# Softplus additions as accumulating transfers, and GpSimd's share of the product with B, in a four-layer network kernel

## The chip, the cores and the metric

The kernel runs on one core of a Trainium2 chip. The metric is the device time of one execution in microseconds (us). The core has five engines that run side by side, each with its own queue in order: TensorE (PE: matrix products, PEld: their weight loads), VectorE (DVE), ScalarE (ACT), GpSimd (POOL) and SyncE (SP, which here only issues DMA transfers). GpSimd issues DMA transfers too. Engines wait for each other and for transfers through semaphores.

## The reference

A feature map of 4 images x 256 channels x 64 x 64 goes through four residual layers, each `x = x + layer(groupnorm(x))`: a deformable convolution, a self-attention, a second deformable convolution with 16 groups, and a Mamba block. The change lies in the last, which is, cut to what matters:

```python
L, D_INNER, D_STATE = 4096, 512, 16                      # L = h * w positions
u, res = split(x_seq @ in_proj_w.T)                      # L x 512 each
u = silu(causal_conv4(u) + conv_b)
dt, Bm, Cm = split(u @ x_proj_w.T)                       # 16 columns each
delta = softplus(dt @ dt_proj_w.T + dt_proj_b)           # L x 512
deltaA = exp(delta[..., None] * A)                       # L x 512 x 16
deltaBu = delta[..., None] * Bm[:, None, :] * u[..., None]
state_t = deltaA_t * state_{t-1} + deltaBu_t             # scan over L
y_t = sum_n state_t[:, n] * Cm_t[n]
out = ((y + u * D) * silu(res)) @ out_proj_w.T
```

## The kernel before, in words

The images are worked off one after the other. For each, the layers `layer0` to `layer3` follow each other; they share only the tile `x`, which holds the image in SBUF (the on-chip memory of 128 partitions). All that follows is about `layer3`.

Positions lie along the free dimension, the 512 inner channels as 4 blocks (`dc`) of 128 partitions. The 4096 positions are cut into 8 chunks (`j`) of 512. In each chunk the 16 states (`n`) are worked off one after the other, so that an image has 128 steps `s = 16 j + n`. A step does this:

- TensorE makes `bn`: row n of B, spread over all partitions by a product with a selecting matrix, in PSUM (L1583). There is one such bank.
- VectorE multiplies it with `du` = delta x u into the tile `h` (`product`, L1598): 128 x 2048 elements. In a helped step it does three of the four blocks only, 128 x 1536; the fourth is `quarter` (L1590) on GpSimd, which reads the row of B from a tile `bs` that SyncE has spread over the partitions by a transfer two steps ahead (`ahead`, L1574), and writes `hq`.
- For each block, ScalarE makes `da = exp(delta x A)` (L1679) in one of two PSUM banks, and VectorE scans with it (L1681), with the running state from `carry`. The fourth scan of a helped step reads `hq` in place of `h`.
- GpSimd saves the scan's last column in `carry` (L1701) and multiplies `h` with the row of C (`cn`, L1704).
- TensorE sums `h` over the states into four PSUM banks `ys` (`add`, L1561), two steps late.

Which steps are helped is the list `helped`: states 14, 15 and 0 to 5, except 14 and 15 of chunk 0.

Beside the states of one chunk, the kernel prepares the next: `front(j)` lays its parts into slots of the steps of chunk j-1, and `close(j)` does the output of the chunk before. The order on TensorE, ScalarE, VectorE and GpSimd is the order in which the program issues the instructions, written out by hand; SyncE's is left to the scheduler. A slot is a pair of step and place in the step (0 and 1 between and after the scans, 2 after the product with C, -1 at the start). Front step k falls on step 16 (j-1) - 5 + k, so on state n = k - 5 of the chunk before; for j = 1, the front starts later and is packed closer.

The part of the front that matters is softplus, computed as relu(z) - (exp(-|z|) ...) with a logarithm. ScalarE writes `du = |z|` and `delta = relu(z)` (L1385, L1386), then `du = exp(-du)` (L1418), `w = du + 1` (L1422), `du = 1 - w` (L1427) and `w = ln(w)` (L1430), each over 128 x 2048. GpSimd adds `du` before and after L1427, which leaves the rounding error of w, and then `w`, to `delta` (L1433, three times), and at last makes `du = delta x u` (L1434), which the next chunk's products read. The first addition must have read `du` before L1427 writes it. For j = 1 the slots are packed closer:

```python
at = dict(e=(11, 0), w=(12, 0), c=(13, 1), ln=(14, 1), s=((11, 0), (12, 1), (15, 0)), sums=(11, 14, 16, 18))
if j == 1:
    at = dict(e=(10, 1), w=(11, 1), c=(12, 1), ln=(13, 0), s=((11, 0), (12, 0), (13, 1)), sums=(10, 12, 13, 15))
```

Here `e`, `w`, `c` and `ln` are the slots of ScalarE's four passes, `sums` the steps of the three additions and of du's product, and `s` those of `split`, which cuts the rows of B into bf16 parts and has a small subtraction on GpSimd twice (L1401, L1405).

The functions that the change touches, with the lines of the profile:

Of the kernel before, what the change touches and what calls it, by code (L numbers as in the profile page):

```python
# [13 lines left out]
ALU = mybir.AluOpType  # L14
# [14 lines left out]
DS = 16  # L29
# [34 lines left out]
class Net:  # L64
# [1068 lines left out]
    def layer3(self, x, out, nxt, early):  # L1133
# [7 lines left out]
        nc, tc = self.nc, self.tc  # L1141
        C = 512
        NC, LEAD = N // C, 5
        with (
# [166 lines left out]
            def front(j):  # L1311


                c = chunks[j]
                todo = []
                put = lambda step, half, pe, rest: todo.append((step, half, pe, rest))
# [112 lines left out]
                put(*at["c"], None, over)  # L1429
                put(*at["ln"], None, lambda: nc.scalar.activation(c["w"], c["w"], AF.Ln))  # L1430

                for step, part in zip(at["sums"], ("du", "du", "w")):
                    put(step, 2, None, lambda part=part: nc.gpsimd.tensor_add(c["delta"], c["delta"], c[part]))  # L1433
                put(at["sums"][3], 2, None, lambda: nc.gpsimd.tensor_mul(c["du"], c["delta"], c["u"]))  # L1434

                for dc in range(4):
# [124 lines left out]
                    nc.tensor.matmul(c["ys", dc], self.ident, h[:, dc, :], start=False, stop=(n == DS - 1))  # L1561


            hs, helped = {}, [s for s in range(NC * DS) if s % DS in (14, 15, 0, 1, 2, 3, 4, 5) and s // 2 != 7]

            def ahead(s):

# [35 lines left out]
            for j in range(1, NC):  # L1603
                for step, half, pe, rest in front(j):
                    at = DS * (j - 1) - (LEAD if j > 1 else 2) + step
                    if at >= 0:
                        slots.setdefault((at, half), []).append((pe, rest))
# [44 lines left out]
            with tc.manual_schedule(  # L1652
# [14 lines left out]
                for s in range(total):  # L1667
                    j, n = s // DS, s % DS
                    c = chunks[j]
# [179 lines left out]
```

## Time and profile before

| what | value |
|---|---|
| median of 3 runs | 9220.24 us (9211.65 to 9221.78) |
| the profiled execution, its own time | 9224.37 us |
| its span, first to last instruction | 9222.6 us |
| mean granted TensorE clock | 0.967 |
| busy: PE, DVE, POOL, ACT | 8204.3, 7308.7, 6976.5, 4967.0 us |
| layer 3 of image 0 (from 1432.1 to 2343.8 us) | 911.7 us |
| an ordinary chunk in it | 112.4 us |
| L1433, 84 additions of 128 x 2048 on GpSimd | 4.54 us each |
| L1590, 248 quarters on GpSimd | 1.27 us each |

The profile comes from one execution. Its page gives each engine's busy time, the groups of instructions by line with their mean duration and the idle time ahead of them, and the DMA queues; further views give single instructions in order of time, and busy times by stretch. A stretch table has, for each stretch, its length, the busy us of PE, PEld, DVE, ACT and POOL with the number of instructions, the granted clock, the share of the DMA engines and GB/s. In a timeline a row has the start, the duration, the engine, the line, the operation, what is written and read, and how many equal instructions were put together. Instructions that only issue a transfer count as no busy time, except for the gathers of layer 0 (L371), which GpSimd issues.

### The profile page before, as it was taken

The page shows a single profiled execution, that of the slowest core. Times are in us where ns is not written, and L with a number is a line of the kernel's source. Part 1 is how long each engine was busy: PE and PEld are TensorE (multiplying, and loading weights), DVE is VectorE, ACT ScalarE, POOL GpSimd, SP SyncE. Part 2 cuts the span into 40 slices and gives each one's busy share as a digit, 9 for nine tenths or more (in the row PEclk, how much of TensorE's full clock was granted, in tenths as well). Part 3 has the DMA queues.
Part 4 walks back from the last instruction along what each step waited for, and adds up shares of the span by engine and source line. Part 5 has one row for each costly group of instructions (what it writes and reads, how often), then busy time and mean ns, then how long its engine had stood idle before and what let it go on. Part 6 is the DMA issues. An engine that isn't in the chain of part 4 may idle for free. (4 is left out here: it accounts for less than half of the span.)

```text
span 9222.6 us, 95498 instructions
## 1 busy us (share of the span) xinstructions
PE 8204.3 (89%) x32023; PEld 4337.2 (47%) x32023; DVE 7308.7 (79%) x8245; ACT 4967.0 (54%) x7717; POOL 6976.5 (76%) x4224
## 2 busy tenths in 40 slices
PE   5889898998888989899888898999988889889997
PEld 4643473443564346344356435634435633564443
DVE  5864498999786458999978645899997854689998
ACT  4843336666684333666668333366666833336664
POOL 4746697998674669799867467889986746788997
PEclk9999999999999999999999999999999999999999
DMA  8930011222892011122389101112248900111221
GB/s 301 356 120 1 29 58 59 67 67 82 288 360 90 1 34 61 56 66 66 100 297 359 61 1 39 59 57 67 66 121 311 349 33 1 43 61 53 63 63 51
DMA packets 409192, 1017.79 MB, mean 110 GB/s; under 512 B 38833, under 2 KB 106834, under 8 KB 406642
## 3 DMA queue, kind: packets, MB, share of 16 engines
q0 software_dynamic: 165888, 604.05, 17.5%
q1 hardware_dynamic: 242802, 407.54, 14.4%
q8 instruction: 255, 4.18, 0.2%
q14 instruction: 247, 2.02, 0.1%
HBM read 849.60 MB, written 88.10 MB: 102 GB/s over the span
## 5 line engine op out<-in xcount | busy, mean ns | idle before, releaser
L1704 POOL TENSOR_TENSOR h<-h,cn 128x2048 f32<-128x2048 f32 x508 | 2300.4, 4528 | 41.1 <-POOL carry L1701 0.2
L1681 DVE TENSOR_TENSOR_SCAN h<-da,carry,h 128x512 f32<-128x512 f32 x1800 | 2175.2, 1265 | 85.0 <-ACT da L1679 36.8
L1679 ACT ACTIVATE da<-delta,l3a 128x512 f32<-128x512 f32 x2048 | 1395.7, 689 | 1206.4 <-DVE h L1681 1202.7
L1561 PE MATMUL y<-h,ident 128*128 128x512 f32 x4096 | 1923.7, 603 | 14.8 <-POOL h L1704 14.8
L371 POOL DMA_INDIRECT g<-tab,idx x1152 | 1337.0, 1161 | 515.3 <-DVE r L380 131.3
L592 POOL TENSOR_TENSOR acc<-acc,e 128x1024 f32<-128x1024 f32 x480 | 1125.4, 2345 | 540.0 <-ACT e L588 518.8
L1561 PEld LDWEIGHTS y<-h,ident 128*128 128x128 f32 x4096 | 787.7, 194 | 1067.6 <-issue 975.9
L415 PE MATMUL pz<-cols,l0w 128*128 128x256 f32 x4608 | 1154.8, 395 | 30.2 <-DVE cols L404 24.5
L489 DVE TENSOR_REDUCE m<-pm 128x3 f32<-128x1536 f32 (+2 forms) x340 | 599.5, 1763 | 699.6 <-PE pm L479 699.6
L380 DVE SCALAR_TENSOR_TENSOR r<-g,wx,r 128x512 f32<-128x512 f32 x1152 | 862.2, 748 | 238.0 <-ACT r L379 230.5
L588 ACT ACTIVATE e<-sc 128x1024 f32<-128x1024 f32 x512 | 496.1, 1020 | 1029.4 <-PE sc L575 1025.2
L1598 DVE TENSOR_TENSOR h<-du,bn 128x2048 f32<-128x2048 f32 (+1 forms) x512 | 1025.9, 2004 | 4.0 <-PE bn L1583 3.9
L599 PE MATMUL cx<-e,v 128*128 128x512 f32 x2048 | 1000.2, 616 | 0.0
L379 ACT ACTIVATE r<-g,wx 128x512 f32<-128x512 f32 x1152 | 830.0, 720 | 283.1 <-DMA g<-tab,idx 230.9
L415 PEld LDWEIGHTS pz<-cols,l0w 128*128 128x128 f32 x4608 | 857.9, 196 | 179.3 <-DVE cols L404 79.4
L888 DVE TENSOR_TENSOR prod<-ring,A 128x768 f32<-128x768 f32 (+1 forms) x640 | 716.6, 1161 | 90.0 <-DMA ring<-ring 59.3
L913 PE MATMUL pacc<-ident,prod 128*128 128x128 f32 x5120 | 678.8, 284 | 75.7 <-POOL prod L893 41.7
L397 PE MATMUL pt<-ident,acc 128*128 128x128 f32 x2304 | 437.2, 290 | 264.3 <-DVE acc L388 261.3
L913 PEld LDWEIGHTS pacc<-ident,prod 128*128 128x128 f32 x5120 | 576.7, 144 | 164.9 <-POOL prod L893 62.2
L599 PEld LDWEIGHTS cx<-e,v 128*128 128x128 f32 x2048 | 352.3, 189 | 599.0 <-issue 596.4
L387 ACT ACTIVATE acc<-r,wy 128x256 f32<-128x256 f32 x1152 | 569.2, 494 | 4.2 <-DVE r L380 3.1
L388 DVE SCALAR_TENSOR_TENSOR acc<-r,wy,acc 128x256 f32<-128x256 f32 x1152 | 551.7, 479 | 2.4 <-ACT acc L387 2.0
(272 smaller groups left out, 11488.7 us busy)
## 6 DMA issues: line engine op xcount, KB each, us to landing
cn<-cd SPq DMA_DIRECT2D x512, 256.0 KB
bs<-cd SPq DMA_DIRECT2D x248, 256.0 KB
tab<-vtnext SPq DMA_DIRECT2D x96, 512.0 KB
ring<-ring SPq DMA_DIRECT2D x288, 126.0 KB
ring<-ring SPq DMA_DIRECT2D x288, 124.0 KB
g<-tab,idx POOLq DMA_INDIRECT x1152, 6.3
tab<-vt SPq DMA_DIRECT2D x28, 640.0 KB
x<-in_x SPq DMA_DIRECT2D x64, 256.0 KB
```

The costliest lines, as they stand in the source:

```text
L371: nc.gpsimd.indirect_dma_start(out=g[:], out_offset=None, in_=tab[:, :], in_offset=bass.IndirectOffsetOnAxis(ap=idx[:, t, k : k + 1], axis=0),
L379: nc.scalar.mul(r, g[:, :, 0, :], wx[:, 0, t, k : k + 1])
L380: nc.vector.scalar_tensor_tensor(r, g[:, :, 1, :], wx[:, 1, t, k : k + 1], r, ALU.mult, ALU.add)
L415: nc.tensor.matmul(sums[m][:, ot, :256], wf[:, i, bass.ts(ot, P)], cols[m][:, i, :], start=(i == 0), stop=(i == 17),)
L592: nc.gpsimd.tensor_add(b["acc"], b["acc"], e)
L599: nc.tensor.matmul(blocks[qb]["cx"], v[:, 4 * (i + kt // 4 * 4) + kt % 4, :], e[:, bass.ts(i % 2, 512)], start=(kt == 0 and i == 0), stop= ...
L913: nc.tensor.matmul(d["pd"][:, ct, t, :], prod[:, x, t, bass.ts(ct, P)], self.ident, is_transpose=True, start=(wy == 0 and x == left[0] and ...
L1561: nc.tensor.matmul(c["ys", dc], self.ident, h[:, dc, :], start=False, stop=(n == DS - 1))
L1598: nc.vector.tensor_mul(h[:, :d, :], c["du"][:, :d, :], c.pop(("bn", n)).to_broadcast([P, d, C]))
L1679: nc.scalar.activation(da, c["delta"][:, dc, :], AF.Exp, scale=al[:, dc, n : n + 1])
L1681: nc.vector.tensor_tensor_scan(h[:, dc, :], da, hb, carry[:, dc, n : n + 1], ALU.mult, ALU.add)
L1704: nc.gpsimd.tensor_mul(h, h, cn.to_broadcast([P, 4, C]))
```

## The change

In the fronts of chunks 2 to 7, the three additions to `delta` become transfers that GpSimd issues, which add their source to what stands in `delta` (`accum_op=ALU.add`), each of 128 x 2048 elements, 1 MB. The front of chunk 1 keeps its three GpSimd additions. The product that makes `du` stays on GpSimd in all. The list of helped steps becomes: in chunks 1 to 7 all states but 13 and 14, in chunk 0 states 0 to 5.

```diff
@@ front(j) of layer3
+                def sum(part):
+                    if j == 1:
+                        nc.gpsimd.tensor_add(c["delta"], c["delta"], c[part])
+                    else:
+                        nc.gpsimd.dma_start(out=c["delta"], in_=c[part], accum_op=ALU.add)
+
                 for step, part in zip(at["sums"], ("du", "du", "w")):
-                    put(step, 2, None, lambda part=part: nc.gpsimd.tensor_add(c["delta"], c["delta"], c[part]))
+                    put(step, 2, None, lambda part=part: sum(part))
                 put(at["sums"][3], 2, None, lambda: nc.gpsimd.tensor_mul(c["du"], c["delta"], c["u"]))
@@ layer3
-            hs, helped = {}, [s for s in range(NC * DS) if s % DS in (14, 15, 0, 1, 2, 3, 4, 5) and s // 2 != 7]
+            hs, helped = {}, [
+                s for s in range(NC * DS) if (s // DS and s % DS not in (13, 14)) or s % DS in (0, 1, 2, 3, 4, 5)
+            ]
```

## The prediction

> **What bounds the kernel now.** I read the page first, then the stretch table cut at the start of each chunk of layer 3, then the timelines of VectorE, ScalarE and GpSimd in one chunk. Only layer 3 is touched, so only it is costed.
>
> ```profile
> L1704 POOL TENSOR_TENSOR h<-h,cn 128x2048 f32<-128x2048 f32 x508 | 2300.4, 4528 | 41.1 <-POOL carry L1701 0.2
> L1681 DVE TENSOR_TENSOR_SCAN h<-da,carry,h 128x512 f32<-128x512 f32 x1800 | 2175.2, 1265 | 85.0 <-ACT da L1679 36.8
> L1679 ACT ACTIVATE da<-delta,l3a 128x512 f32<-128x512 f32 x2048 | 1395.7, 689 | 1206.4 <-DVE h L1681 1202.7
> ```
>
> In these groups ScalarE waits 1202.7 us for VectorE's scans, while the scans waited 85 us for anything. The waiting goes towards VectorE. The stretch table (busy us of PE, PEld, DVE, ACT, POOL, count in brackets) says the same by chunk; the first two rows are ordinary chunks, the last is chunk 7 of image 0:
>
> ```profile
> 1887.20:1999.50 112.30, 106.70 (x253) 45.82 (x252) 110.84 (x87) 73.93 (x102) 105.26 (x49) 1.00 0.23 66
> 1999.50:2111.90 112.40, 106.81 (x253) 45.81 (x252) 110.94 (x87) 73.94 (x102) 105.37 (x49) 1.00 0.22 67
> ...
> 2224.30:2343.80 119.50, 89.64 (x243) 39.70 (x243) 114.72 (x99) 73.72 (x108) 88.34 (x42) 0.91 0.57 171
> ```
>
> VectorE is busy 110.9 of 112.4 us; the 1.5 us left are the 0.1 us between product and first scan, 16 times. It bounds the chunk. TensorE has 5.6 us idle, GpSimd 7.0, at a granted clock of 1.00.
>
> What a state costs VectorE, with and without GpSimd's quarter (the 128x1536 and the 128x2048 product):
>
> ```profile
> 1810.79 1.73 DVE L1598 TENSOR_TENSOR h<-du,bn 128x1536 f32<-128x1536 f32 x1
> 1812.62 3.63 DVE L1681 TENSOR_TENSOR_SCAN h<-da,carry,h 128x512 f32<-128x512 f32 x3
> 1816.17 1.26 DVE L1681 TENSOR_TENSOR_SCAN h<-da,carry,hq 128x512 f32<-128x512 f32 x1
> 1817.34 2.26 DVE L1598 TENSOR_TENSOR h<-du,bn 128x2048 f32<-128x2048 f32 x1
> 1819.71 4.81 DVE L1681 TENSOR_TENSOR_SCAN h<-da,carry,h 128x512 f32<-128x512 f32 x4
> 1824.43 2.26 DVE L1598 TENSOR_TENSOR h<-du,bn 128x2048 f32<-128x2048 f32 x1
> ```
>
> From product to product: 1817.34 - 1810.79 = 6.55 us with help, 1824.43 - 1817.34 = 7.09 without. A helped state is worth 0.53 us.
>
> Below, n is a state's number in its chunk and Tn the end of its last scan. In this chunk the 1817.34 product is n=6, so T6 is 1824.5. The front's step k falls on n = k-5 (LEAD): additions at n = 6, 9, 11, du's product at n = 13.
>
> **The change part by part.**
>
> *Helped states.* Chunk 0 keeps its six. Chunks 1 to 7 go from 8 helped states (0-5, 14, 15) to 14 (0-12, 15). That is 6 more in 28 chunks, 168 in all. 168 x 0.53 = 89 us off VectorE, all on the path as long as VectorE bounds: an ordinary chunk would go to 112.4 - 3.2 = 109.2 us.
>
> *GpSimd.* It gains 6 quarters at 1.27 us (L1590) and loses 3 additions at 4.54 (L1433), in chunks 1 to 6. Each transfer costs it an issue; the nearest row is the gather's, 1161 ns, with some 0.3 us before the next. Per chunk: 105.3 + 7.6 - 13.6 + 3 x 1.4 = 103.5 us occupied of 109.2. It keeps room. By state: mul 4.53 + carry 0.2 + quarter 1.27 = 6.0 against 6.56. The states with an issue, a split subtraction (1.15, n=6 and 7) or du's product (4.53, n=13) run over; summing these, its lag peaks near 3.5 us at n=13-15. Quarter n+1 is wanted only at the fourth scan, about 5.3 us after Tn, so no stall. n=13 and 14, where du falls, are left unhelped. Chunk 7 has no transfers and plenty of GpSimd time (88 of 119.5).
>
> *SP.* Each extra helped state adds a 256 KB row broadcast (bs), 168 x 256 KB, on a queue that issues one in 0.32 us two states (13 us) ahead. Its buffer comes free with the quarter two states before. The DMA share is 0.22: nothing on the path.
>
> *The transfers: what must wait now.* The first addition was an instruction of GpSimd; now it lands some time after its issue. Three things wait: ScalarE's L1427, which overwrites du that the first transfer still reads; the second and third transfers, on GpSimd, for the one before; du's product and the next chunk's first exponential, for the third. L1427 is the tight one:
>
> ```profile
> 1824.92 4.54 POOL L1704 TENSOR_TENSOR h<-h,cn 128x2048 f32<-128x2048 f32 x1
> 1829.41 4.54 POOL L1433 TENSOR_TENSOR delta<-delta,du 128x2048 f32<-128x2048 f32 x1
> ...
> 1837.10 0.59 ACT L1461 COPY x<-front 128x512 f32<-128x512 f32 x1
> 1837.58 2.00 ACT L1427 ACTIVATE du<-w,ones 128x2048 f32<-128x2048 f32 x1
> 1839.49 1.29 ACT L1679 ACTIVATE da<-delta,l3a 128x512 f32<-128x512 f32 x2
> ...
> 1838.61 2.26 DVE L1598 TENSOR_TENSOR h<-du,bn 128x2048 f32<-128x2048 f32 x1
> 1840.98 4.81 DVE L1681 TENSOR_TENSOR_SCAN h<-da,carry,h 128x512 f32<-128x512 f32 x4
> ```
>
> L1427 starts at 1837.58, 1.1 us before T8 (1838.7), and behind it on ScalarE stand the exponentials that n=9's scans need. The first is done at 1840.18, and the scan starts at 1840.98, behind its product: 0.8 us of room. With the shorter product of n=9 it is 0.3. So L1427 may start up to T8 - 0.8, and as n=7 and 8 now take 13.1 us, that is T6 + 12.3. Later than that, VectorE stalls one for one, and nothing gives it back.
>
> The transfer's issue: in the trace mul n=6 ends at T6 + 4.9. In the new order quarter 7 and the split subtraction stand before carry 6, 7.4 us after T5, so carry 6 slips 0.8 us past T6 and mul 6 ends near T6 + 5.6. The transfer has 12.3 - 5.6 = **6.7 us** from issue to landing. The room of the others: 1 to 2 has three states less the lag (over 15 us), 2 to 3 over 12, the third to du's product about 11, with 4 us more before the next chunk wants du.
>
> *How long an accumulating transfer takes.* No row shows one. The nearest are the gathers, issued from GpSimd too:
>
> ```profile
> DMA to landing us min/median/max: 4.2/6.3/8.0
> ...
> q0 software_dynamic: 165888, 604.05, 17.5%
> ```
>
> The minimum is an unqueued gather of 0.5 MB. Packets take 17.5% x 9222.6 / 1152 = 1.4 us of it, so 2.8 is fixed, and 1 MB takes 2.8 us of packets. Low bound, at copy rate: 2.8 + 2.8 = 5.6 us, no stall at all (and a gain beyond the 89 has no source). If the destination must be read as well, at the same rate, 2.8 + 5.6 = 8.4. The Trainium skill's *DMA: Bandwidth & Descriptors* calls the adding unit an elementwise reduce of two streams ("SDMA does more than copy"), which is for the second. The arithmetic may be slower still; half that rate, 2.8 + 11.2 = 14.0, is my high end. I take **8.0**: near the doubled end, a little under because both sides are SBUF where the gather reads scattered rows of HBM. Stall: 8.0 - 6.7 = 1.3 us in each of 24 chunks (1 to 6), 31 us.
>
> *Two rules weighed.* The same page's "Anatomy of one DMA" gives 2.0 us + bytes / 436 GB/s: 4.4 for 1 MB, which would leave no stall and the sum at -89. But for 0.5 MB it gives 3.2 where the trace's fastest gather has 4.2, so the trace is used. Against the change speaks its "SWDGE vs HWDGE vs iDMA": GpSimd writes the descriptors to SBUF, and VectorE's 2-port mode locks it out meanwhile. If an issue had to wait out a 1.7 us product, the first transfer would land that much later: 24 x 1.7 = 41 us more, the sum at -17. The trace shows no such lock here: beside a VectorE 99% busy, L1704 takes 4503 to 4556 ns and the quarter 1253 to 1301. I charge nothing.
>
> *Sum.* -89 + 31 = -58. Against the profiled run's 9224.4 us (span 9222.6): 9166; the median shown, 9220.2, is 4.1 below that run, so **9162**, 0.6% faster. A measurement of this kernel can tell about 0.2% (18 us) from no change.
>
> **The rivals.**
>
> *No stall: 9131.* The transfer lands within 6.7 us and all 89 us come. For: the copy-rate bound of 5.6. Against: two operands to read, and broadcasts on the same engines.
>
> *TensorE takes over: about 9167.* It is busy 106.8 us a chunk, part of its idle time is waits for ScalarE (L1379 for L1386) that don't shrink, and 109.2 leaves 2.4. If it holds the chunk at 110.5, the gain is 1.9 x 28 = 53 us. For: 98% busy is hard for a queue in order. Against: the helped states n=15 to 1 run at 6.56 us with TensorE full already, and at n=7 and 10 it waits about 1 us for VectorE's product, which is cover.
>
> *Slower: the transfer's own rate.* One mechanism, at L1427: each us beyond 6.7 costs 24. From 6.7 + 89/24 = **10.4 us** on the change loses. At 14.0 the stall is 7.3 x 24 = 175, net +86: 9306. For: no row shows the adding rate, and the wait stands ahead of a saturated engine. Against: 10.4 needs a rate well under half of the gather's. Beyond about 11 us du's product would wait for the third transfer too.
>
> That the change does nothing can be left out: the built order has the transfers and the quarters in it.
>
> **How the numbers follow.** Forecast (landing between 6.7 and 9.6 us) 0.38; no stall 0.18; TensorE 0.08: faster by over 0.2% in all of these, 0.64. Landing between 9.6 and 11.2 us puts it within 0.2%: 0.09. Slower transfers: 0.27. The range starts just under the case without a stall, 9128, and reaches up to 9280, a landing of about 12.7 us; beyond lies most of the rest of the slow case. The faster cases alone span 9128 to 9202.
>
> **What would show it.** Products of n=6 to 12 with 1536 elements and 6.56 us from one to the next; L1590 x416; chunks 1 to 6 near 110.5 us, chunk 7 shorter by 3; L1433 x12; a row of GpSimd DMA issues x72 with a landing near 8 us; a wait of ScalarE's L1427 for that DMA of 1 to 2 us. Wrong if the wait is longer than 3.7 us a chunk, if GpSimd waits before du's product or the second transfer, if the quarters or L1704 got longer beside the transfers, or if VectorE's idle time now ends on TensorE's bn.

## The result, and the profile after

The changed kernel takes 9234.6 us (median of 17; 9215.2 to 9254.7), the kernel before, run alongside on the same chip, 9220.0 (median of 17). The ratio is 1.0019, with a 95% interval from 1.0011 to 1.0027: slower by 0.2%, 14.5 us. The forecast was 9162, 0.6% faster. The two profiled executions differ by 2.2 us only (9226.6 against 9224.4), so what follows is read from layer 3 alone: its stretches in the four images add up to 3631.7 us before and 3649.7 after, 18.0 us more, which is the size of the measured loss. (The other layers, which the change does not touch, happened to be 15.8 us shorter in the execution that was profiled.)

The page, costliest groups after (busy and mean, then the idle time before the group and what ended it):

```profile
L1712 POOL TENSOR_TENSOR h<-h,cn 128x2048 f32<-128x2048 f32 x508 | 2300.2, 4528 | 41.2 <-POOL carry L1709 0.2
L1689 DVE TENSOR_TENSOR_SCAN h<-da,carry,h 128x512 f32<-128x512 f32 x1632 | 1981.9, 1267 | 165.9 <-ACT da L1687 122.4
L1687 ACT ACTIVATE da<-delta,l3a 128x512 f32<-128x512 f32 x2048 | 1392.1, 689 | 1093.9 <-DVE h L1689 1089.7
...
L1598 POOL TENSOR_TENSOR hq<-du,bs 128x512 f32<-128x512 f32 x416 | 544.4, 1309 | 64.9 <-DMA bs<-cd 44.1
```

The quarters are there (L1598, 416 for 248). What they took off VectorE came back as waiting: the scans wait 165.9 us where they waited 85.0, and 122.4 of it is ended by ScalarE's exponentials (36.8 before). A new wait has appeared on GpSimd: 44.1 us for `bs`.

The stretch table after, for two ordinary chunks and chunk 7 of image 0:

```profile
1774.50:1886.90 112.40, 107.00 (x254) 46.11 (x253) 107.95 (x88) 74.00 (x102) 101.88 (x55) 1.00 0.39 108
1886.90:1998.90 112.00, 106.42 (x253) 45.82 (x252) 107.73 (x87) 73.97 (x102) 101.76 (x55) 1.00 0.40 109
...
2224.50:2349.00 124.50, 89.52 (x239) 39.64 (x238) 112.89 (x99) 73.65 (x108) 93.96 (x48) 0.88 0.62 189
```

VectorE's work in a chunk fell from 110.9 to 107.8 us, as it should, and these two chunks stayed at 112: VectorE is idle 4.4 us of them now. Chunks 1, 2 and 5 of this image take 113.5 us, for a reason that follows. Chunk 7 grew from 119.5 to 124.5.

The ScalarE pass that overwrites `du`, by its own line, and the transfers by theirs (issue times on GpSimd, then the time from issue to landing):

```profile
L1427 ACT ACTIVATE du<-w,ones x28: 2002/2002/2005, 1509.7 to 9044.7; 128x2048 f32<-128x2048 f32 x28
...
  DMA delta<-du: 64.1, 24
```

```profile
L1436 POOL DMA_DIRECT2D delta<-du x48: 854/872/1000, 1601.2 to 9057.0; - x48
...
DMA to landing us min/median/max: 8.4/8.8/10.5
```

L1427 waits for the first transfer in every one of the 24 chunks, 2.67 us on average. What that does is seen in chunk 2 of image 0, first on ScalarE, then on VectorE. Here T6 is 1710.46 and T8 1723.58; the product that starts at 1723.49 is n=9's:

```profile
1725.33 2.00 ACT L1427 ACTIVATE du<-w,ones 128x2048 f32<-128x2048 f32 x1 [2.77 <-DMA delta<-du]
1727.24 1.28 ACT L1687 ACTIVATE da<-delta,l3a 128x512 f32<-128x512 f32 x2
...
1732.76 0.58 ACT L1297 COPY sres<-front 128x512 f32<-128x512 f32 x1 [1.62 <-PE front L1293]
1733.24 1.91 ACT L1430 ACTIVATE w<-w 128x2048 f32<-128x2048 f32 x1
1735.05 1.29 ACT L1687 ACTIVATE da<-delta,l3a 128x512 f32<-128x512 f32 x2
```

```profile
1723.49 1.73 DVE L1606 TENSOR_TENSOR h<-du,bn 128x1536 f32<-128x1536 f32 x1
1727.95 3.63 DVE L1689 TENSOR_TENSOR_SCAN h<-da,carry,h 128x512 f32<-128x512 f32 x3 [2.73 <-ACT da L1687]
...
1732.67 1.73 DVE L1606 TENSOR_TENSOR h<-du,bn 128x1536 f32<-128x1536 f32 x1
1735.77 3.76 DVE L1689 TENSOR_TENSOR_SCAN h<-da,carry,h 128x512 f32<-128x512 f32 x3 [1.37 <-ACT da L1687]
```

L1427 starts at 1725.33 = T6 + 14.87, the two exponentials of n=9 stand behind it, and the scan waits 2.73 us for them. From product to product n=9 takes 9.18 us instead of 6.56.

A second stall follows at n=10: the gate's copy L1297 waits 1.62 us for TensorE's projection, and L1430 and again the exponentials stand behind that copy, so that n=10 takes 7.95 us here. It comes in 12 of the 24 chunks, and these differ from the others in TensorE's granted clock. In all 24, the late copy before it leaves TensorE idle. In chunk 2, TensorE then gets half the clock for 3.4 us, and the projection takes 3.62 us; in chunk 4, after a wait of about the same length, the clock stays and it takes 1.98 us. First TensorE in the two chunks, then the stretch table for the 3.4 us in question:

```profile
1729.10 3.62 PE L1293 MATMUL front<-xn,l3a 128*128 128x512 f32 x4 [2.56 <-ACT sres L1297]
...
1954.95 1.98 PE L1293 MATMUL front<-xn,l3a 128*128 128x512 f32 x4 [2.50 <-ACT sres L1297]
```

```profile
1729.02:1732.43 3.41, 3.33 (x4) 1.51 (x5) 3.41 (x4) 1.41 (x3) 2.21 (x2) 0.50 0.24 81
1954.30:1957.71 3.41, 2.76 (x7) 1.33 (x8) 3.41 (x4) 2.70 (x6) 2.84 (x2) 1.00 0.23 83
```

The 12 chunks with such a stretch late in n=9 have n=10 at 7.75 to 7.99 us, the 12 without have it at 6.55 to 6.67. What decides which chunks get it was not tried.

Against the expectation that each helped state is 0.53 us shorter (-89), the states of layer 3 lost 97 us. The periods from state to state place them: n=9 60.1, n=10 15.9, n=6 8.6, chunk 7 15.1, less 2.6 in chunk 0. That leaves the states 8.1 us longer than before; a tail of 3.3 us behind the last scan of images 0 to 2 makes 18.0.

**n=6.** It takes 6.92 us instead of the 6.56 of a helped state in all 24 chunks. On ScalarE, beside its product (1817.01 to 1818.74), and on VectorE:

```profile
1817.77 0.61 ACT L1399 CAST bp<-dbc 64x512 bf16<-64x512 f32 x1
1818.39 0.61 ACT L1400 CAST bt<-dbc 64x512 bf16<-64x512 f32 x1
1819.03 1.91 ACT L1418 ACTIVATE du<-du 128x2048 f32<-128x2048 f32 x1
1820.85 1.28 ACT L1687 ACTIVATE da<-delta,l3a 128x512 f32<-128x512 f32 x2
```

```profile
1818.85 2.46 DVE L1689 TENSOR_TENSOR_SCAN h<-da,carry,h 128x512 f32<-128x512 f32 x2
1821.56 1.28 DVE L1689 TENSOR_TENSOR_SCAN h<-da,carry,h 128x512 f32<-128x512 f32 x1 [0.25 <-ACT da L1687]
```

Two casts and the exponential, 3.1 us, stand between the second and the third `da`. They fitted beside a product of 2.26 us; beside one of 1.73 the third scan waits.

**Chunk 7.** In images 0 to 2 the next image's table is written in this chunk. SyncE's queue, then GpSimd and VectorE near its end:

```profile
2307.49 12.15 SPq L1543 DMA_DIRECT2D tab<-vtnext  x8
2319.74 2.64 SPq L1582 DMA_DIRECT2D cn<-cd  x2
2322.47 13.08 SPq L1543 DMA_DIRECT2D tab<-vtnext  x8
2335.66 1.49 SPq L1582 DMA_DIRECT2D cn<-cd  x1
2337.19 1.33 SPq L1582 DMA_DIRECT2D bs<-cd  x1
```

```profile
2343.04 1.26 POOL L1598 TENSOR_TENSOR hq<-du,bs 128x512 f32<-128x512 f32 x1 [9.22 <-DMA bs<-cd]
```

```profile
2344.34 1.28 DVE L1689 TENSOR_TENSOR_SCAN h<-da,carry,hq 128x512 f32<-128x512 f32 x1 [2.91 <-POOL hq L1598]
2349.18 1.23 DVE L1714 TENSOR_TENSOR h<-h,cn 128x1024 f32<-128x1024 f32 x1 [3.56 <-POOL carry L1709]
```

Eight table transfers hold SyncE's queue 12 to 13 us, about 1.6 each, and the row broadcast `bs` is issued behind them, so GpSimd waits 9.2 us for it. Of the 15.1 us that chunk 7 lost in its states, 8.5 are at n=15, where the last scan waits so; 3.0 are at n=5, by a hold of VectorE that is shown below (after c1); the rest was not taken apart. Image 3, which writes no table, takes 108.0 us in its chunk 7 (111.2 before): the whole 3.2 us of six helped states.

### The profile page after: what moved, and what is told of

Its sections match the earlier page's. It is cut to its first block, busy times and chain, and to the rows that moved or that the text cites. A ratio compares the mean times of both kernels' runs of the same rounds, so it can differ in the third digit from the quotient of the medians.

```text
span 9224.8 us, 96083 instructions
## 1 busy us (share of the span) xinstructions
PE 8219.7 (89%) x32023; PEld 4351.1 (47%) x32023; DVE 7227.5 (78%) x8245; ACT 4969.2 (54%) x7717; POOL 6909.3 (75%) x4392
## 3 DMA queue, kind: packets, MB, share of 16 engines
q0 software_dynamic: 176256, 679.56, 21.6%
q1 hardware_dynamic: 266994, 451.59, 15.9%
## 5 line engine op out<-in xcount | busy, mean ns | idle before, releaser
L1712 POOL TENSOR_TENSOR h<-h,cn 128x2048 f32<-128x2048 f32 x508 | 2300.2, 4528 | 41.2 <-POOL carry L1709 0.2
L1689 DVE TENSOR_TENSOR_SCAN h<-da,carry,h 128x512 f32<-128x512 f32 x1632 | 1981.9, 1267 | 165.9 <-ACT da L1687 122.4
L1606 DVE TENSOR_TENSOR h<-du,bn 128x1536 f32<-128x1536 f32 (+1 forms) x512 | 936.6, 1829 | 4.5 <-PE bn L1591 4.4
L1598 POOL TENSOR_TENSOR hq<-du,bs 128x512 f32<-128x512 f32 x416 | 544.4, 1309 | 64.9 <-DMA bs<-cd 44.1
```

The lines of the kernel that those rows point to most:

```text
L1606: nc.vector.tensor_mul(h[:, :d, :], c["du"][:, :d, :], c.pop(("bn", n)).to_broadcast([P, d, C]))
L1689: nc.vector.tensor_tensor_scan(h[:, dc, :], da, hb, carry[:, dc, n : n + 1], ALU.mult, ALU.add)
L1712: nc.gpsimd.tensor_mul(h, h, cn.to_broadcast([P, 4, C]))
```

## The experiments

The runs were spread over several chips; on those of the a and b runs the kernel before took 9419 us, on that of the c runs 9213, so only ratios to the kernel before on the same chip are compared. Theory: the gain is on VectorE as forecast, and the first transfer lands too late for L1427; n=6 and chunk 7 are losses of their own. Rivals: transfers slow the engines' access to SBUF; GpSimd or TensorE bounds the chunk; the quarters are worth less than 0.53 us.

**a1: the first transfer earlier.** It goes into the slot within n=6, ahead of the product with C (in chunks 1 to 6).

```diff
-for step, part in zip(at["sums"], ("du", "du", "w")):
-    put(step, 2, None, lambda part=part: sum(part))
+for k, (step, part) in enumerate(zip(at["sums"], ("du", "du", "w"))):
+    put(step, 1 if k == 0 and j > 1 else 2, None, lambda part=part: sum(part))
```

> The changed kernel with the first transfer of a chunk issued ahead of carry and the product with C of n=6 (slot 1 of that step, not slot 2), in the fronts of chunks 2 to 7. It then lands about 5 us earlier. Theory (the transfer's landing holds L1427 on ScalarE, and that costs VectorE 60 us at n=9 and 16 us at n=10): landing near T6 + 10, ahead of T6 + 12.3, so both stalls go, n=9 and n=10 take 6.56 us, and the time falls by about 76 us below the changed kernel, to some 61 below the kernel before (ratio 0.9934). Rival (TensorE, at 98% in a shorter chunk, is what holds n=9 and n=10, and L1427 only shows it): the stall moves to bn or the banks and at most 20 us come back (ratio near 1.000). Rival (transfers slow the engines by their traffic): n=9 and n=10 keep most of their excess, at other states.

Measured: 0.9934 [0.9920, 0.9948]. Its stretch table, two ordinary chunks:

```profile
1710.93:1820.47 109.54, 106.40 (x253) 45.83 (x252) 107.83 (x88) 73.84 (x102) 101.64 (x55) 1.00 0.42 111
1820.47:1930.12 109.65, 106.52 (x253) 45.82 (x252) 107.93 (x87) 73.84 (x102) 101.64 (x55) 1.00 0.42 111
```

The work of every engine is that of the changed kernel, and the chunk is 2.5 us shorter. The issue is at T6 + 0.45, L1427 no longer waits, n=9 and n=10 take 6.56 us, n=6 still 6.92. So one transfer issued 4.9 us sooner is worth 0.85%, 78 us (0.9934 / 1.0019, give or take 15 by the two intervals); the account above has 76 for n=9 and n=10. No chunk from 1 to 6 has the half clock near n=9 any more, so the stall at n=10 was a consequence of that at n=9, by way of TensorE's idle time. The transfers as such cost no more than their lateness.

**a2: chunk 7 of images 0 to 2 helped as before.**

```diff
+if nxt is not None:
+    helped = [s for s in helped if s < DS * (NC - 1) or s % DS < 6 or s % DS == 15] + [DS * NC - 2]
```

> The changed kernel with chunk 7 of images 0 to 2 helped as before (states 0 to 5, 14, 15). Theory (there the bs broadcasts stand behind the next image's table transfers in SyncE's queue, and GpSimd waits up to 9 us for them): chunk 7 goes back to about 119.5 us from 124.5, 5 us for each of three images, so 15 us below the changed kernel (ratio 1.000 to the kernel before). Rival (chunk 7's loss is ScalarE's or TensorE's work for the table, which the quarters only shift): less than 5 us come back (ratio 1.0015).

Measured: 0.9998 [0.9990, 1.0007], 0.2% below the changed kernel (19 us; the account has 15 + 10). Chunk 7 is back at 119.1 to 119.7 us.

**a3 and a4: each half alone.** a3 is the kernel before with the new list of helped states, so its additions are on GpSimd; a4 is the changed kernel with the old list.

```diff
# a3, against the kernel before
-s for s in range(NC * DS) if s % DS in (14, 15, 0, 1, 2, 3, 4, 5) and s // 2 != 7
+s for s in range(NC * DS) if (s // DS and s % DS not in (13, 14)) or s % DS in (0, 1, 2, 3, 4, 5)
# a4, against the changed kernel
-s for s in range(NC * DS) if (s // DS and s % DS not in (13, 14)) or s % DS in (0, 1, 2, 3, 4, 5)
+s for s in range(NC * DS) if s % DS in (14, 15, 0, 1, 2, 3, 4, 5) and s // 2 != 7
```

> The new list of helped states alone, all additions on GpSimd. Theory: GpSimd becomes the bound in chunks 1 to 6: 105.3 + 7.6 = 112.9 us of work against 109.2 for VectorE, so a chunk takes 113 us or more, 0.5 to 1.5 us longer than before, and chunk 7 loses as in the changed kernel: 20 to 50 us slower than before (ratio 1.002 to 1.005). Rival (GpSimd's idle 7 us a chunk is room enough, and the transfers bring nothing): chunks near 110.5 us, 20 to 40 us faster than before (0.996 to 0.998).

> The transfers alone, with the old list of helped states. Theory (only L1427's date matters): the transfer is issued at T6 + 5.0, lands about 9 us later, and L1427 may start up to T8 - 0.3 = T6 + 13.9 here, as n=7 to 9 are long. Stall 0 to 0.5 us a chunk: 0 to 12 us slower than before (ratio 1.000 to 1.0013). Rival (the traffic of 72 MB slows engines or other transfers): over 40 us slower (1.004 and up), spread over the states 6 to 13.

Measured for a3: 1.0109 [1.0094, 1.0125], well above what was expected; chunks 2 to 6 of images 0 to 2 take about 116 us. What its quarter waits for, then who waits for the quarter:

```profile
  DMA bs<-cd: 41.9, 6
...
  DVE h L1683: 154.9, 52
```

VectorE waits 154.9 us for quarters, in two places of each chunk: n=11 takes about 9.9 us and n=15 9.7. The expectation summed GpSimd's work over the chunk (105.3 + 7.6 = 112.9 us); but the scans ask for a quarter within a state, and GpSimd's lag behind an addition is worked off only several states later. And the wait for `bs` in chunk 7 is there without any accumulating transfer (41.9 us, 6 times), so it belongs to the helped list alone.

Measured for a4: 0.9999 [0.9991, 1.0008]. L1427 waits 24.6 us in all, as with unhelped states n=7 and n=8 it is wanted 1 us later; the loss at n=9 is about 0.5 us in images 0 to 2 and none in image 3. Neither half gains: the quarters need the room on GpSimd that the transfers make.

**b1: a1 and a2 together.**

> The first transfer issued in slot 1 of n=6 (as in a1), and chunk 7 of images 0 to 2 helped as before (as in a2). Theory (the two losses are separate and add): a1's ratio 0.9934 less some 15 us of chunk 7: 0.9918, chunks 1 to 6 at 109.4 us (108.4 in image 3), chunk 7 of images 0 to 2 at 119.4. Rival (chunk 7's loss shrinks once the chunks before are undisturbed): no better than a1, 0.993.

Measured: 0.9916 [0.9902, 0.9930]. Its interval overlaps that of a1, but its layer 3 is 17 us shorter than a1's in the trace. The two losses add.

**b2: is it the queue that makes chunk 7 slow?** a1, with the later `bs` transfers of that chunk issued from ScalarE's queue, past SyncE's.

```diff
+late = name == "bs" and nxt is not None and j == NC - 1 and n > 5
-nc.sync.dma_start(
+(nc.scalar if late else nc.sync).dma_start(
```

> As a1, all 14 states of chunk 7 helped, but in chunk 7 of images 0 to 2 the bs broadcasts of n=6 to 15 are issued from ScalarE's queue, where the table's transfers don't stand ahead of them. Theory (SyncE's queue, 12 to 13 us for each eight table transfers, makes bs late): GpSimd no longer waits for bs, chunk 7 falls from 121 to about 116 us, and its late tail goes: 20 to 25 us less than a1, ratio 0.991. Rival (the DMA engines, 62% busy there, are late themselves): GpSimd still waits 5 us and more for bs, the ratio stays near a1's 0.9934. ScalarE's own issues cost it under 1 us each either way.

Measured: 0.9933 [0.9919, 0.9947], no better than a1: a miss. GpSimd's wait for `bs` is gone, and so is the tail, so the queue did cause those. But chunk 7 still takes 121.3 us in images 0 and 1 and 123.8 in image 2, because a new wait came up (the waits of image 0's chunk):

```profile
ACT da L1688 <- POOL carry L1710: 3.4, 1, 3.4
```

The inference is that ScalarE's issue waits for a `bs` buffer to come free on GpSimd, with exponentials behind it; n=11 takes 8.0 to 9.3 us and n=13 9.4 to 10.7. Moving the issue moved the wait.

**b3: n=14 helped too in chunks 1 to 6, and in chunk 7 of image 3** (b1 with the list's `not in (13, 14)` cut to `!= 13`).

> As b1, and n=14 helped too in chunks 1 to 6 (and chunk 7 of image 3). 24 states of 0.53 us are to be had, 13 us. Theory (VectorE bounds, GpSimd's lag after du's product leaves about 0.5 us before quarter 15 is wanted): 10 to 13 us below b1, ratio 0.9905, n=14 at 6.56. Rival (the lag is over: du's product and two quarters in a row): VectorE waits for quarter 15 or the next chunk's quarter 0, n=15 above 6.56, no gain or a loss against b1.

Measured: 0.9909 [0.9893, 0.9924]; n=14 takes 6.56 us with no new wait in these chunks, which take 109.0. GpSimd had room for one more quarter.

**b4: the first split a slot later,** so that its two casts leave the place beside n=6's product (b1 with this edit).

```diff
-s=((11, 0), (12, 1), (15, 0))
+s=((11, 1), (12, 1), (15, 0))
```

> As b1, with the two bf16 copies of the first split (0.61 us each) in slot 1 of n=6 in place of slot 0, where they stand ahead of the 1.9 us exponential L1418. Theory (n=6 takes 6.92 us in place of 6.56 because L1418 and the two copies no longer fit beside the shorter product): n=6 goes to 6.56, 24 x 0.36 = 9 us below b1, ratio 0.991. Rival (L1418 alone is too long there, or the copies now hold up n=7): n=6 plus n=7 stay at 13.5 us, no gain.

Measured: 0.9910 [0.9895, 0.9925]; n=6 takes 6.56 us, n=7 also. b3 and b4 differ from b1 by less than the intervals; their verdict rests on the periods. (Chunk 7 of two images lost about 5 us each in both, see after c1.)

**c1: all four edits.**

> First transfer in n=6's early slot, chunk 7 of images 0 to 2 helped as before the change, n=14 helped too, first split a slot later. If the four are independent, the gains of the last two (0.53 us for n=14, 0.36 us for n=6, in chunks 1 to 6 of four images: 13 and 9 us) come on top of the 0.84% of the first two: ratio to the kernel before 0.989 to 0.990, n=6 and n=14 both at 6.56 us, chunks 1 to 6 at 108.7 us (image 3: 107.5). If TensorE (106.9 us of work a chunk) or GpSimd begins to bound, chunks stay at 109.0 and new waits of VectorE for GpSimd's quarter or for TensorE's bn appear; ratio 0.991.

Measured: 0.9903 [0.9886, 0.9919], just short of the 0.989 to 0.990 that was expected; the lowest ratio of all, though within the intervals of b1, b3 and b4. All of its interval lies below the kernel before. Its stretch table:

```profile
1655.80:1764.42 108.62, 106.16 (x253) 45.82 (x252) 107.16 (x87) 73.89 (x102) 102.91 (x56) 1.00 0.45 115
1764.42:1873.15 108.73, 106.27 (x253) 45.83 (x252) 107.27 (x87) 73.89 (x102) 102.87 (x56) 1.00 0.42 115
```

Image 3 has 107.4 in each of its chunks 1 to 6, with every state but n=2, n=3 and n=13 at 6.56 us. TensorE's 106.2 us of work fit into that, so TensorE does not bound even here.

What c1 lacks is, in its profiled execution, in chunk 7. In a4 (one image), b3, b4 and c1 (two images each) its state n=6, counted from last scan to last scan, takes 13.2 us. GpSimd and VectorE there, image 1 of c1:

```profile
4512.24 4.50 POOL L1714 TENSOR_TENSOR h<-h,cn 128x2048 f32<-128x2048 f32 x1
4512.86 3.90 DVE L1511 SCALAR_TENSOR_TENSOR known<-gm,rs 128x2 f32<-128x2 f32 x1
```

A small VectorE instruction for the next image, L1511, starts after GpSimd's product and ends with it. In these seven cases it takes 3.9 to 4.5 us; in the 29 others of the twelve traces, where that product does not start ahead of it, at most 0.18. The chunks 7 of b3, b4 and c1 are thereby 9 to 10 us longer in all than those of b1, most of what b3 and b4 had gained elsewhere. In the changed kernel, L182, another such instruction, is held in the same way behind a quarter at n=5 of chunk 7 (1.15 us in place of 0.16). No run changed this order.

**c2: copying in place of adding.** The changed kernel with the transfers as plain copies: it leaves the three sums out and serves for timing alone.

```diff
-nc.gpsimd.dma_start(out=c["delta"], in_=c[part], accum_op=ALU.add)
+nc.gpsimd.dma_start(out=c["delta"], in_=c[part])
```

> The changed kernel with its transfers as plain copies of du and w onto delta, without the addition (the three sums are left out in chunks 1 to 7). If the reading of the destination is what doubles the packet time (the prediction's second bound), a copy of 1 MB lands 2.5 to 3 us sooner: median 5.6 to 6.3 us from issue to landing, packet time of the software queue lower by about 2.6 us a transfer, L1427 starts near T6+12, n=9 takes 6.56 to 6.8 us instead of 9.2, n=10 6.56, and the kernel is at 0.992 to 0.994 of the kernel before. If the time is that of 1 MB through this queue whatever is done with it, it lands at 8.4 us as the adding one, n=9 stays at 9.2 us and the ratio at 1.002.

Measured: 0.9940 [0.9922, 0.9958]. Its transfers by their line, then the page's row of that queue (packets, MB, share of 16 engines):

```profile
L1436 POOL DMA_DIRECT2D delta<-du x48: 573/586/623, 1600.1 to 8985.2; - x48
...
DMA to landing us min/median/max: 5.9/6.1/8.3
```

```profile
q0 software_dynamic: 176256, 679.56, 19.8%
```

The same row of the changed kernel has the same packets and bytes at 21.6%:

```profile
q0 software_dynamic: 176256, 679.56, 21.6%
```

Less the gathers' 1614 us (17.5% of 9222.6, from the kernel before), packets take (21.6% x 9224.8 - 1614) / 72 = 5.3 us for a transfer that adds and (19.8% x 9154.2 - 1614) / 72 = 2.8 us for one that copies. The landing falls from 8.8 to 6.1 us by about as much. L1427 then starts at T6 + 12.0, n=9 and n=10 take 6.56 us, and the kernel stands where a1 does. The adding all but doubles the packet time, and what it adds is the stall. (The gathers are taken to cost the same in all three kernels. GpSimd's issue is 0.3 us shorter too.)

## Why the prediction was wrong

**Right.** VectorE bounds the chunk, and a helped state is worth 0.53 us wherever nothing else waits (6.56 against 7.09). The first transfer is the tight one: issue forecast at T6 + 5.6, found at T6 + 5.3; the start that L1427 may not pass forecast at T6 + 12.3, confirmed by a1 and c2 (T6 + 12.0, no stall) and by the stall of n=9 here, which is 14.87 - 12.3 to within 0.1 us. The second and third transfers, and du's product, held nobody up. The rival of TensorE as the bound falls with c1; TensorE enters only by the 12 stretches of half clock. The lock of GpSimd by VectorE, which the Trainium skill raises (*DMA: Bandwidth & Descriptors*, "SWDGE vs HWDGE vs iDMA") and the prediction charged nothing for, does not show: the issue takes 872 ns in the median, beside a VectorE that is busy almost throughout. (Whether VectorE's instructions here use that mode, no run shows.) Nor did the transfers slow other engines where it counts: L1712 still has a mean of 4528 ns. The quarter behind each first and second transfer does take 1.56 to 1.65 us in place of 1.27, one of the prediction's signs of being wrong, but no scan waits for these 48; in c2, with copies, none is longer than 1.31.

**The term that was mis-sized.** Landing 8.0 us, stall 1.3 us, 31 us in all. Measured: 8.8 in the median, and 9.5 from issue to L1427's start for the first of the three in images 0 to 2; stall 2.5 us at n=9 in the mean of the 24 chunks, 60 us. The prediction had the right composition as its middle bound (8.4: the destination is read too, packets 5.6 us; c2 has 5.3) and then went below it because both ends are SBUF. A plain copy between them lands in 6.1 us, over the 5.6 worked out from the gathers, so there was no such discount: the packets were about right, the part around them is 3.5 us and not 2.8. The Trainium skill's *DMA: Bandwidth & Descriptors*, "Anatomy of one DMA", 2.0 us + bytes / 436 GB/s, gives 4.4 us for 1 MB, which is under the plain copy's 6.1 and half of the adding one's 8.8.

**That term alone does not turn the sign.** With 60 in place of 31 the sum is -29, still 0.3% faster. The rival of the slow transfer had the mechanism and the place, but its break-even of 10.4 us was not reached. Three omitted terms did the rest.

- n=10, 16 us. The prediction had VectorE stall "one for one" and read TensorE's clock as 1.00. But the late ScalarE pass also left TensorE idle 2.5 us, in half of the chunks its clock then halved for 3.4 us, and a copy that waited for the slower projection stood in front of the next exponentials: 12 times 1.35 us. With that, the transfer cost 76 of the 89 us.
- Chunk 7, about 25 us (15 in states, 10 in the tail) in place of part of the gain. That it "has no transfers and plenty of GpSimd time" was so, and beside the point; that SyncE has "nothing on the path" was judged from the DMA share of ordinary chunks (0.22), while in chunk 7 SyncE's queue holds table transfers of 12 us a batch in front of the broadcasts. That part was not looked at.
- n=6, 9 us. Shortening VectorE's product shortens the cover of what ScalarE does beside it.

Sum: -89 + 60 + 16 + 25 + 9, less 3 in chunk 0, is +18, which is layer 3's measured growth.

**Open.** Why chunk 7 of images 0 to 2 stays at 121 us and more with the `bs` wait removed (b2) is settled only in part: n=11 and n=13 lose to the moved issue, and n=5 1.0 us to the hold of L182; n=4 to n=7 take 7.7 to 8.7 us, as they did in part before the change, and their waits were not taken apart. Nor was it tried why the first transfer of a chunk takes 0.7 us longer than the median. In images 0 to 2 a load of the next image (`x<-in_x`, L1483) is issued 0.5 us after it each time, and it lands in 9.2 to 10.5 us; in image 3, which has no such load, it lands in 8.7 to 8.9. That fits the load as the cause and does not show it.

## What to carry to other kernels

When work is moved from an engine to a transfer, the engine's time is not the price; the price is the delay until the first reader or overwriter may go on, and behind that wait stands whatever the waiting engine has queued. Give the transfer its place by its landing, not by the slot of the instruction that it replaces: here the same transfer, issued 4.9 us earlier, turned +0.2% into -0.7%. Where a bounding engine gets faster, look in every stage (also the odd last one) at what was hidden beside it, and at the queue that feeds the new work. And read the granted clock behind every new wait of TensorE: here the idle time alone cost VectorE nothing at n=10, the half clock behind it 16 us.

## What was not expected of the hardware

- A transfer that adds 1 MB from SBUF to SBUF takes 8.4 to 10.5 us from issue to landing (8.8 in the median), one that copies it 5.9 to 8.3 (6.1). The packet time is 5.3 against 2.8 us, some 3.4 us around it in both.
- GpSimd's issue of the adding transfer takes 872 ns, of the copy 586.
- Table transfers issued from SyncE take its queue about 1.6 us each (eight in 12.2 to 13.1 us), against 0.32 us for a row broadcast in quiet stretches.
- After a wait of about 2.5 us, TensorE's granted clock fell to 0.50 for 3.4 us in 12 of 24 chunks; in chunk 2 of image 0 four products took 3.62 us, where they take 1.98 at 1.00.
- A VectorE instruction of 128 x 2 elements took 3.9 to 4.5 us in place of 0.18, ending with the GpSimd product that had started ahead of it (seven cases in a4, b3, b4 and c1), while scans and products on VectorE ran beside such products at their usual length.
